# An adder convolution whose sums of maxima move from VectorE to accumulating DMAs

## The chip, the cores and the metric

The kernel runs on one core of a Trainium2 chip, as one launch. The metric is the device time of that launch in microseconds (us). The engines are named as in the profile: PE multiplies matrices, PEld loads its weights, DVE (VectorE) and ACT (ScalarE) work element by element, POOL (GpSimd) and SP issue DMAs here, and 16 DMA engines move what they issue.

## The reference

Four layers follow each other on `x` of 8 images, 64 channels, 128 x 128 pixels, each as `x = x + layer(groupnorm(x))`. The change touches the first, an adder convolution: a 3 x 3 convolution with the absolute difference in place of the product, then bias and relu.

```python
patches = conv_general_dilated_patches(x, (3, 3), (1, 1), [(1, 1), (1, 1)])
P = patches.transpose(0, 2, 3, 1).reshape(-1, C * 9)
wf = w.reshape(O, -1)
def per_out(wrow, bi):
    return relu(bi - abs(P - wrow[None, :]).sum(-1))
```

So each of 64 output channels needs, at each pixel, 9 x 64 absolute differences of the input and a weight, and their sum. The other three layers are a spline activation, a wavelet convolution and a nearest codebook vector.

## The kernel before

**Tiling.** Two images share the 128 partitions (64 channels each), which makes four pairs of images. `layer0` handles one pair: four chunks of 32 rows, padded to 34 x 130 in SBUF, and for each chunk four groups of 16 output channels. One chunk and one group are a pass; a pair has 16 passes. Within a pass each output channel `m` needs its nine taps. A tile is the term of one or more taps for one `m`: a 128 x 4096 buffer, of which PE sums the channels with 16 matmul records (line 722).

**Kinds of tile.** A string of letters gives each `m` its tiles in order. `A` is one tap's absolute difference, one ACT operation (line 653). The others use |x - w| = 2 max(x, w) - x - w, with a matmul weight of 2 (`sel2`); the linear rest is added per pass by the matmuls of `linear` (line 616). `D` is one tap's maximum, one DVE operation (line 655). `C` is the sum of two taps' maxima: the maximum of the first (655) and two fused maximum-and-add operations of half a tile each (659). `T` is the same with three taps. A fused tile saves PE a tile and costs DVE three operations instead of two. `PLANS` holds four tables of such strings; `PLANS[0]` is used in all 16 passes of the first pair and in the last two passes of each later pair, whose other passes use plans 3, 1 and 2 because layers two and three of the pair before run beside them (`layer2_beside`, `layer3_beside`).

**Order.** The order on PE, ACT and DVE is the written one (`manual_schedule`); POOL's and SP's is left to the framework's scheduler. The loop at line 703 takes two tiles a step. Before each tile's matmuls it fills every buffer in `free` with the next tiles' terms (`terms`, lines 705 to 710), so the number of buffers is the distance that DVE and ACT may run ahead of PE. After the matmuls the buffer goes back (line 723). Then come the step's chores: load of the next chunk into one of the free buffers 24 steps before it begins, its normalization 8 steps before, `relu` at the end of a pass, eight residual adds after it (line 633, DMAs from POOL that accumulate 64 KB each into `y`), and `finish` 14 steps after the end (statistics and stores). In the first pair there are seven buffers of the padded size beside `x0`, which holds the first chunk; one of the eight always holds the current chunk.

**Setup.** Before the first pair, `raw_norm` loads the first pair in eight pieces of 1 MB through three buffers, DVE takes their statistics, and then the weights of the later layers are prepared.

Of the kernel before, what the change touches and what calls it, by code (L numbers as in the profile page):

```python
# [21 lines left out]
P = 128  # L22
C = 64
# [3 lines left out]
RA = 32  # L27
# [8 lines left out]
M = 16  # L36
OG = C // M
NP = H // RA * OG
LATER = 8
BUFS_ALONE, BUFS_BESIDE = 8, 7  # L40

SPAN = {"A": 1, "D": 1, "C": 2, "T": 3}
PLANS = (
    (
        "AADDACAD",
        "DADAACAD",
        "DADACADA",  # L50
        "ADADDCAA",
        "DAACADAD",
        "DDAADCAA",
        "DADDAADC",
        "DADAADDDD",
    ),
    (
        "ACAACAA",
# [28 lines left out]
        "ACAAAT",  # L87
        "AAAACAC",
        "AAADCAC",
    ),  # L90
)
assert all(sum(SPAN[k] for k in kinds) == 9 for plan in PLANS for kinds in plan)
# [8 lines left out]
class Net:  # L101
# [21 lines left out]
    def setup(self, w0, b0, coef, sbase, ssp, bias1, dw_w, dw_b, pw_w, pw_b, cv_w, cv_b, embed):  # L123
# [54 lines left out]
        self.ones = ct([C, P], "ones")  # L178
        nc.gpsimd.memset(self.ones, 1.0)
        self.mhalf = ct([P, 1], "mhalf")  # L180
        nc.gpsimd.memset(self.mhalf, -0.5)

# [6 lines left out]
        self.b0 = ct([P, len(PLANS), OG], "b0")  # L189
        with tc.tile_pool(name="setup", bufs=1) as sp, tc.tile_pool(name="setup_ps", bufs=2, space=PSUM) as pp:  # L190
            w0o = sp.tile([P, OG, C, 9], F32, name="w0o")
            braw = sp.tile([P, OG], F32, name="braw")
            with nc.allow_non_contiguous_dma("weights, once"):
                for i in range(2):
# [167 lines left out]
            self.b2c = ct([P, 2], "b2c")  # L362
            for oab in range(2):
                bp = pp.tile([P, 1], F32, name="bp", tag="tp")
                nc.tensor.matmul(bp, self.gam[0:C, oab, :], self.ones[:, 0:1], start=True, stop=True)
# [15 lines left out]
            nc.tensor.matmul(ep, self.ones, esq, start=True, stop=True)  # L381
            self.esq_half = ct([P, NE], "esq_half")
            nc.scalar.mul(self.esq_half, ep, 0.5)

# [43 lines left out]
    def raw_norm(self, pair, mr):  # L428

        stats = self.stats_tile()  # L430
        with self.tc.tile_pool(name="raw", bufs=3) as pool:
            for j in range(NCH):
                t = pool.tile([P, R * W], F32, name="raw")
                self.nc.sync.dma_start(out=t, in_=self.x_dram[pair][:, j * R * W : (j + 1) * R * W])
                yield
                self.tile_stats(stats, 4 * j, t)
                yield
        with self.tc.tile_pool(name="raw_ps", bufs=1, space=PSUM) as pp:
            yield from self.group_norm_steps(stats, mr, pp)
# [103 lines left out]
    def layer0(self, pair, mr, stats, bufs, beside):  # L543
# [9 lines left out]
        with ExitStack() as ctx:  # L553
            bp = ctx.enter_context(tc.tile_pool(name="l0_bufs", bufs=1))
            sp = ctx.enter_context(tc.tile_pool(name="l0", bufs=1))
            pp = ctx.enter_context(tc.tile_pool(name="l0_ps", bufs=1, space=PSUM))
            ctx.enter_context(tc.manual_schedule(engines={ET.PE, ET.Activation, ET.DVE}))
            free = deque(bp.tile([P, (RA + 2) * (W + 2)], F32, name=f"buf{n}") for n in range(bufs - 1))
            held, xps, pss, sums, sxs, sts, ys, xr = {}, {}, {}, {}, {}, {}, {}, []
# [6 lines left out]
            def load(j):  # L566
                held[j] = free.popleft()
                xps[j] = self.load_chunk(pair, j, held[j])

            def pad(j):  # L570
                at = self.chunk_rows(xps[j], j)[2]
                self.normalize(at, at, mr)

            def tap(j, t, h=None):
                lo, n = (0, RA) if h is None else (h * RA // 2, RA // 2)
# [71 lines left out]
            def terms(p, m, kind, ts):  # L647
                j, o = divmod(p, OG)
                w = self.w0[:, o * M + m, :]
                buf = free.popleft()  # L650
                ab = buf[:, 0 : RA * W].rearrange("p (r w) -> p r w", w=W)
                if kind == "A":
                    nc.scalar.activation(ab, tap(j, ts[0]), AF.Abs, bias=w[:, ts[0] : ts[0] + 1], scale=-1.0)  # L653
                else:
                    nc.vector.tensor_scalar(ab, tap(j, ts[0]), w[:, ts[0] : ts[0] + 1], None, ALU.max)  # L655
                    for h in range(2):
                        at = ab[:, h * RA // 2 : (h + 1) * RA // 2, :]
                        for t in ts[1:]:
                            nc.vector.scalar_tensor_tensor(at, tap(j, t, h), w[:, t : t + 1], at, ALU.max, ALU.add)  # L659
                return buf, ab  # L660

            tiles, first = [], [0]
            for p in range(NP):
# [33 lines left out]
            held[0] = self.x0  # L697
            xps[0] = self.x0.rearrange("p (r w) -> p r w", w=W + 2)
            chores[-24].clear()
            chores[-8].clear()  # L700
            made = {}
            coming = iter(range(len(tiles)))
            for step in range(max(chores) + 1):
                for n in range(2 * step, min(2 * step + 2, len(tiles))):
                    while free:
                        k = next(coming, None)
                        if k is None:
                            break
                        p, m, kind, ts = tiles[k]
                        made[k] = terms(p, m, kind, ts)  # L710
                        if k - LATER in first[OG::OG]:
                            free.append(held.pop(p // OG - 1))
# [3 lines left out]
                    buf, ab = made.pop(n)  # L716
                    sel = self.sel if kind == "A" else self.sel2
                    for q in range(2):
                        for g in range(NG):
                            rhs = ab[:, RA // 2 * q + 4 * g : RA // 2 * q + 4 * g + 4, :]  # L720
                            at = pss[p][2 * M * g : 2 * M * (g + 1), q, :]
                            nc.tensor.matmul(at, sel[:, M - 1 - m : 3 * M - 1 - m], rhs, start=(n == first[p]), stop=(n + 1 == first[p + 1]))  # L722
                    free.append(buf)
                for f, *a in chores.pop(step, ()):
                    f(*a)

# [579 lines left out]
    def run(self):  # L1306
        tc = self.tc
        mr, later = self.mr0, None
        for pair in range(self.n_pairs):
            last = pair + 1 == self.n_pairs  # L1310
            stats, nxt = self.stats_tile(), self.mr_tile()
            raw, count = (iter(()), 2) if last else (self.raw_norm(pair + 1, nxt), 2 * NCH + 8)
            plans = [3] + [1] * 7 + [2] * 6 + [0] * 2 if later else [0] * NP
            counts = [TILES[n] // 2 if n else 0 for n in plans[:-2]] + [count // 2] * 2
            if later is None:
                self.layer0(pair, mr, stats, BUFS_ALONE, lambda p: (plans[p], raw, counts[p]))
            else:
                with tc.tile_pool(name="between", bufs=1) as bp:
                    between = bp.tile([P, NCH * 4, 6], F32, name="between")
                    steps = chain(self.layer2_beside(later, between, sum(counts[:8])), self.layer3_beside(between, pair - 1, sum(counts[8:-2])), raw)  # L1320
                    self.layer0(pair, mr, stats, BUFS_BESIDE, lambda p: (plans[p], steps, counts[p]))
            if last:
                self.first.close()
            else:
# [42 lines left out]
```

## Time and profile before

| | us |
|---|---|
| median of three runs | 19169.5 (19165.1 to 19175.5) |
| the profiled execution: span from first to last instruction | 19147.4 |
| first matmul of the first pair | 143.7 |
| relu (line 620) of its first and last pass, 15 passes apart | 378.3 and 3788.2 |
| one residual add in the first pair, issue to landing, median | 3.9 |

The span is that of one execution, and the run's time also holds what lies around it, some 22 us. In the page, busy time is the share in which an engine worked on an instruction; the records of PE overlap, so its busy share says where PE had work and not that it worked at its peak. A group's row gives busy time, the mean of one, and the idle time before it with what ended that idle time. The chain of waits is followed back from the last instruction, at each step to what released it.

### The profile page before, as it was taken

How to read it: one execution, taken by the hardware profiler on the slowest of the kernel's cores; microseconds unless marked ns; L12 is line 12 of the kernel's file. 1: busy time of each engine (PE TensorE's matmuls, PEld its weight loads, DVE VectorE, ACT ScalarE, POOL GpSimd, SP SyncE). 2: the span in 40 equal slices, each digit the busy share in tenths (PEclk: the TensorE clock that was granted, in tenths of full speed). 3: DMA queues.
4: the chain of work that ended last, by engine and by line, in shares of the span. 5: the costliest groups of instructions: out<-in, count | busy, mean ns of one | idle time of the engine just before them, and what ended most of it. 6: DMA issues, size and time to landing. Idle time of an engine off the chain costs nothing.

```text
span 19147.4 us, 330733 instructions
## 1 busy us (share of the span) xinstructions
PE 18332.0 (96%) x146698; PEld 5818.3 (30%) x146698; DVE 17951.2 (94%) x13918; ACT 17340.8 (91%) x6457; POOL 2778.2 (15%) x1663
## 2 busy tenths in 40 slices
PE   8999999999999999999999999999999999999977
PEld 2333233232233222222222322222232323222263
DVE  8999999989999999998999999999899999999867
ACT  7999999889999999988999999998899999999803
POOL 0000000000000244300000034420000003442005
PEclk9999999999999999999999999999999999999986
DMA  2000000121111001021111100002011110000231
GB/s 66 6 11 10 6 10 8 40 68 32 40 34 33 25 18 29 25 61 48 34 42 30 33 21 24 23 28 78 29 35 41 35 34 16 22 25 13 62 96 39
DMA packets 425513, 636.07 MB, mean 33 GB/s; under 512 B 65168, under 2 KB 314640, under 8 KB 399120
## 3 DMA queue, kind: packets, MB, share of 16 engines
q1 hardware_dynamic: 368272, 549.81, 9.5%
q0 software_dynamic: 55808, 65.11, 1.9%
q8 instruction: 1149, 18.83, 0.4%
q14 instruction: 284, 2.33, 0.0%
HBM read 485.16 MB, written 129.54 MB: 32 GB/s over the span
## 4 chain that ended last, share of the span: by engine, by line
PE 53%; DVE 28%; issue 10%; ACT 8%; DMA 1%; SPq 0%; POOL 0%; DVEq 0%; ACTq 0%; POOLq 0%
PE ps L722 39%; DVE buf L655 12%; DVE buf L659 9%; ACT buf L653 7%; PE cv L1139 5%; PE pa L818 2%; PE pb L818 2%; DVE dw L1116 1%; DVE nd L1264 1%; DVE ix L1266 1%; DVE dw L897 1%; PE py L1162 1%; DVE x L655 1%; ACT t L1254 1%; PE pd L1252 1%
## 5 line engine op out<-in xcount | busy, mean ns | idle before, releaser
L722 PE MATMUL ps<-buf,sel 128*32 128x512 f32 x116336 | 13030.5, 597 | 371.1 <-DVE buf L659 234.2
L653 ACT ACTIVATE buf<-buf,w 128x4096 f32<-128x4096 f32 x1980 | 7213.9, 3710 | 301.8 <-PE ps L722 295.3
L653 ACT ACTIVATE buf<-x,w 128x4096 f32<-128x4096 f32 x1938 | 7046.2, 3710 | 347.0 <-PE ps L722 288.0
L722 PEld LDWEIGHTS ps<-buf,sel 128*32 128x32 f32 x116336 | 3625.9, 110 | 9365.5 <-issue 7898.4
L655 DVE TENSOR_SCALAR buf<-buf,w 128x4096 f32<-128x4096 f32 x1795 | 4162.2, 2356 | 188.7 <-PE ps L722 187.5
L655 DVE TENSOR_SCALAR buf<-x,w 128x4096 f32<-128x4096 f32 x1558 | 3639.5, 2366 | 287.4 <-PE ps L722 271.2
L659 DVE SCALAR_TENSOR_TENSOR buf<-buf,w,buf 128x2048 f32<-128x2048 f32 x1262 | 2913.4, 2348 | 22.9
L659 DVE SCALAR_TENSOR_TENSOR buf<-x,w,buf 128x2048 f32<-128x2048 f32 x1072 | 2475.3, 2349 | 19.7
L1267 POOL DMA_INDIRECT g<-in_L_conv_embed_weight,ix x768 | 1832.8, 2386 | 2840.3 <-issue 1400.3
L633 POOL DMA_DIRECT2D y<-in_x x480 | 608.8, 2099 | 9431.2 <-ACT y L620 6457.2
L1139 PE MATMUL cv<-dw,w2s 64*128 64x512 f32 x6912 | 1654.0, 606 | 3.2 <-issue 3.2
L653 ACT ACTIVATE x<-buf,w 128x4096 f32<-128x4096 f32 x396 | 1468.9, 3709 | 59.3 <-PE ps L722 59.3
L722 PE MATMUL ps<-x,sel 128*32 128x512 f32 x10832 | 1303.0, 594 | 27.1 <-DVE x L659 18.5
L1139 PEld LDWEIGHTS cv<-dw,w2s 64*128 64x128 f32 x6912 | 627.4, 186 | 1025.4 <-issue 1011.1
L655 DVE TENSOR_SCALAR x<-buf,w 128x4096 f32<-128x4096 f32 x281 | 659.9, 2348 | 24.6 <-PE ps L722 24.4
L722 PEld LDWEIGHTS ps<-x,sel 128*32 128x32 f32 x10832 | 350.8, 110 | 851.1 <-issue 747.5
L1116 DVE SCALAR_TENSOR_TENSOR dw<-sub,dws,dw 128x512 f32<-128x512 f32 (+2 forms) x768 | 574.5, 748 | 10.6
L1264 DVE CUSTOM_DVE_ANT_0 nd<-pd,t 128x512 f32<-128x512 f32 x768 | 519.8, 677 | 31.0 <-ACT t L1254 31.0
L807 DVE TENSOR_TENSOR r<-r,r 128x1024 f32<-128x1024 f32 x384 | 454.9, 1218 | 80.2 <-ACT r L806 72.2
L1266 DVE FIND_INDEX8 ix<-best,nd 128x8 uint32<-128x512 f32 x768 | 526.1, 685 | 0.1
L1252 PE MATMUL pd<-embT,xn 64*128 64x512 f32 x1536 | 490.1, 650 | 29.1 <-DVE best L1264 28.7
L1254 ACT ACTIVATE t<-esq_half,xsq 128x512 f32<-128x512 f32 x768 | 510.8, 717 | 3.1 <-DVE best L1264 3.1
(239 smaller groups left out, 7891.7 us busy)
## 6 DMA issues: line engine op xcount, KB each, us to landing
w2s<-w_dram SPq DMA_DIRECT2D x576, 192.0 KB
xd<-x_dram SPq DMA_DIRECT2D x256, 256.0 KB
x<-x_dram SPq DMA_DIRECT2D x56, 1024.0 KB
u<-u_dram SPq DMA_DIRECT2D x64, 768.0 KB
raw<-in_x SPq DMA_DIRECT2D x32, 1024.0 KB
x_dram<-y SPq DMA_DIRECT2D x512, 64.0 KB
out<-x SPq DMA_DIRECT2D x32, 1024.0 KB
y<-in_x POOLq DMA_DIRECT2D x480, 64.0 KB, 4.2
```

The source lines that it names most:

```text
L653: nc.scalar.activation(ab, tap(j, ts[0]), AF.Abs, bias=w[:, ts[0] : ts[0] + 1], scale=-1.0)
L655: nc.vector.tensor_scalar(ab, tap(j, ts[0]), w[:, ts[0] : ts[0] + 1], None, ALU.max)
L659: nc.vector.scalar_tensor_tensor(at, tap(j, t, h), w[:, t : t + 1], at, ALU.max, ALU.add)
L722: nc.tensor.matmul(at, sel[:, M - 1 - m : 3 * M - 1 - m], rhs, start=(n == first[p]), stop=(n + 1 == first[p + 1]))
L818: nc.tensor.matmul(to[images[i], q, :], dspl[:, k, ws[i], :], cubes[i][:, cols], start=(p == 0), stop=stop)
L1116: nc.vector.scalar_tensor_tensor(out, v, wt, out, ALU.mult, ALU.add)
L1139: nc.tensor.matmul(ps[:, i], weights[r, w // 3, :], v, start=(k == 0 and n == 0), stop=(k == 3 and n == 8))
L1252: nc.tensor.matmul(ps, xns[j][at, r, :], self.embT[at, :], start=True, stop=True)
L1254: nc.scalar.activation(t, self.esq_half, AF.Identity, bias=xsqs[j][:, n : n + 1])
L1264: nc.vector.tensor_tensor_reduce(nd, ps, t, 1.0, -FAR, ALU.subtract, ALU.max, mx[:, 0:1])
L1266: nc.vector.max_index(ix, mx, nd)
L1267: nc.gpsimd.indirect_dma_start(out=g[:, img, :], out_offset=None, in_=self.embed, in_offset=bass.IndirectOffsetOnAxis(ap=ix[:, 0:1], axis=0),)
```

## The change

The first pair gets a new kind of tile, `M`, also the sum of two taps' maxima. DVE computes both maxima into two buffers, and POOL issues a DMA that adds the second buffer into the first, within SBUF. `M` tiles are issued 8 places earlier than their own, and their second buffer is given back 8 tiles after use.

```diff
-BUFS_ALONE, BUFS_BESIDE = 8, 7
+AHEAD = 8
+PADDED = (RA + 2) * (W + 2)
+TERMS_ALONE, TERMS_BESIDE = 8, 5
-SPAN = {"A": 1, "D": 1, "C": 2, "T": 3}
+SPAN = {"A": 1, "D": 1, "C": 2, "M": 2, "T": 3}
 PLANS = (
     (
-        "AADDACAD",
...
+        "DAADDAMA",
+        "DACAAMD",
...
@@ raw_norm
-        with self.tc.tile_pool(name="raw", bufs=3) as pool:
+        with self.tc.tile_pool(name="raw", bufs=2) as pool:
@@ layer0
-            ctx.enter_context(tc.manual_schedule(engines={ET.PE, ET.Activation, ET.DVE}))
-            free = deque(bp.tile([P, (RA + 2) * (W + 2)], F32, name=f"buf{n}") for n in range(bufs - 1))
+            ctx.enter_context(tc.manual_schedule(engines={ET.PE, ET.Activation, ET.DVE, ET.Pool}))
+            free = deque(bp.tile([P, PADDED], F32, name="wide") for n in range(1))
+            free.extend(bp.tile([P, RA * W], F32, name=f"buf{n}") for n in range(bufs))
...
+            def release(buf):
+                if waiting and buf.shape[1] == PADDED:
+                    j = waiting.pop()
+                    held[j] = buf
+                    xps[j] = self.load_chunk(pair, j, buf)
+                else:
+                    free.append(buf)
...
+                def maxima(t):
+                    buf = free.popleft()
+                    ab = buf[:, 0 : RA * W].rearrange("p (r w) -> p r w", w=W)
+                    nc.vector.tensor_scalar(ab, tap(j, t), w[:, t : t + 1], None, ALU.max)
+                    return buf, ab
+
+                if kind == "M":
+                    (buf, ab), (other, _) = maxima(ts[0]), maxima(ts[1])
+                    into, of = (b[:, 0 : RA * W].rearrange("p (h n) -> p h n", h=2) for b in (buf, other))
+                    nc.gpsimd.dma_start(out=into, in_=of, accum_op=ALU.add, max_dma_last_dim=8192)
+                    return buf, ab, other
...
-                        (begin - 24, load),
-                        (begin - 8, pad),
+                        (begin - 32, waiting.append),
+                        (begin - 12, pad),
...
-            coming = iter(range(len(tiles)))
+            coming = deque(sorted(range(len(tiles)), key=lambda k: k - AHEAD * (tiles[k][2] == "M")))
...
-                    while free:
-                        k = next(coming, None)
-                        if k is None:
-                            break
+                    while coming and len(free) > (tiles[coming[0]][2] == "M"):
+                        k = coming.popleft()
...
-                    free.append(buf)
+                    release(buf)
+                    spare[n + LATER] = other
+                    if spare.get(n) is not None:
+                        release(spare.pop(n))
@@ run
-            plans = [3] + [1] * 7 + [2] * 6 + [0] * 2 if later else [0] * NP
+            plans = [3] + [1] * 7 + [2] * 6 + [4] * 2 if later else [0] * NP
```

The new `PLANS[0]` has 16 strings, one for each `m`: 58 `A`, 42 `D`, 6 `C` and 16 `M` in a pass, 122 tiles. The old one has 60 `A`, 56 `D` and 14 `C`, 130 tiles; it stays as `PLANS[4]` for the last two passes of the later pairs. The term buffers lose the padding, so that nine fit (eight small ones and one of two padded buffers, of which the other holds the chunk); the next chunk is loaded into the padded buffer that comes free. POOL's order becomes the written one too. In setup, the tile `ones` moves from the constants to a pool that is closed after setup.

More of the change, by code (lines that the diff above doesn't have):

```diff
@@ L39 @@
 LATER = 8
-BUFS_ALONE, BUFS_BESIDE = 8, 7
-SPAN = {"A": 1, "D": 1, "C": 2, "T": 3}
+AHEAD = 8
+PADDED = (RA + 2) * (W + 2)
+TERMS_ALONE, TERMS_BESIDE = 8, 5
+SPAN = {"A": 1, "D": 1, "C": 2, "M": 2, "T": 3}
 PLANS = (
     (
-        "AADDACAD",
[L49 to L55, printed above, removed]
+        "DAADDAMA",
+        "DACAAMD",
+        "ADAADADM",
+        "DDAAAMAD",
+        "ACAMADD",
+        "ADADAMDA",
+        "DAADMAC",
+        "AAMDADDA",
+        "AMADDADA",
+        "ACMADAA",
+        "DADAMDAD",
+        "DDAADMAA",
+        "DADMACA",
+        "DAAMDADA",
+        "ACMDAAD",
+        "DAADDAAM",
     ),
@@ L89 @@
         "AAADCAC",
+    ),
+    (
+        "AADDACAD",
+        "DADAACAD",
+        "DADACADA",
+        "ADADDCAA",
+        "DAACADAD",
+        "DDAADCAA",
+        "DADDAADC",
+        "DADAADDDD",
     ),
@@ L177, in setup @@
         nc.vector.tensor_reduce(self.reorder[:, :, M : 2 * M], ident.rearrange("p (g i m) -> p i m g", g=NG, i=2), AX.X, ALU.add)
-        self.ones = ct([C, P], "ones")
-        nc.gpsimd.memset(self.ones, 1.0)
         self.mhalf = ct([P, 1], "mhalf")
@@ L191, in setup @@
             w0o = sp.tile([P, OG, C, 9], F32, name="w0o")
+            ones = sp.tile([C, P], F32, name="ones")
+            nc.gpsimd.memset(ones, 1.0)
             braw = sp.tile([P, OG], F32, name="braw")
@@ L364, in setup @@
                 bp = pp.tile([P, 1], F32, name="bp", tag="tp")
-                nc.tensor.matmul(bp, self.gam[0:C, oab, :], self.ones[:, 0:1], start=True, stop=True)
+                nc.tensor.matmul(bp, self.gam[0:C, oab, :], ones[:, 0:1], start=True, stop=True)
                 nc.vector.tensor_tensor(self.b2c[:, oab : oab + 1], bp, b2[:, 1, oab : oab + 1], ALU.add)
@@ L380, in setup @@
             ep = pp.tile([P, NE], F32, name="ep", tag="ep")
-            nc.tensor.matmul(ep, self.ones, esq, start=True, stop=True)
+            nc.tensor.matmul(ep, ones, esq, start=True, stop=True)
             self.esq_half = ct([P, NE], "esq_half")
@@ L556, in layer0 @@
             pp = ctx.enter_context(tc.tile_pool(name="l0_ps", bufs=1, space=PSUM))
-            ctx.enter_context(tc.manual_schedule(engines={ET.PE, ET.Activation, ET.DVE}))
-            free = deque(bp.tile([P, (RA + 2) * (W + 2)], F32, name=f"buf{n}") for n in range(bufs - 1))
-            held, xps, pss, sums, sxs, sts, ys, xr = {}, {}, {}, {}, {}, {}, {}, []
+            ctx.enter_context(tc.manual_schedule(engines={ET.PE, ET.Activation, ET.DVE, ET.Pool}))
+            free = deque(bp.tile([P, PADDED], F32, name="wide") for n in range(1))
+            free.extend(bp.tile([P, RA * W], F32, name=f"buf{n}") for n in range(bufs))
+            padded, waiting, held, xps, pss, sums, sxs, sts, ys, xr = set(), [], {}, {}, {}, {}, {}, {}, {}, []
             plan = [beside(p)[0] for p in range(NP)]
@@ L564, in banks @@
                 return pp.tile([P, 2, NE], F32, name=f"ps{p % 2}", tag=f"ps{p % 2}")
-            def load(j):
-                held[j] = free.popleft()
-                xps[j] = self.load_chunk(pair, j, held[j])
+            def release(buf):
[5 more added lines that the diff above has]
+                    free.append(buf)
             def pad(j):
@@ L572, in pad @@
                 self.normalize(at, at, mr)
+                padded.add(j)
             def tap(j, t, h=None):
@@ L649, in terms @@
                 w = self.w0[:, o * M + m, :]
+                assert j in padded
+                def maxima(t):
[8 more added lines that the diff above has]
+                    return buf, ab, other
                 buf = free.popleft()
@@ L659, in terms @@
                             nc.vector.scalar_tensor_tensor(at, tap(j, t, h), w[:, t : t + 1], at, ALU.max, ALU.add)
-                return buf, ab
+                return buf, ab, None
             tiles, first = [], [0]
@@ L698, in layer0 @@
             xps[0] = self.x0.rearrange("p (r w) -> p r w", w=W + 2)
-            chores[-24].clear()
-            chores[-8].clear()
-            made = {}
-            coming = iter(range(len(tiles)))
+            chores[-32].clear()
+            chores[-12].clear()
+            padded.add(0)
+            made, spare = {}, {}
+            coming = deque(sorted(range(len(tiles)), key=lambda k: k - AHEAD * (tiles[k][2] == "M")))
+            n_made = 0
             for step in range(max(chores) + 1):
                 for n in range(2 * step, min(2 * step + 2, len(tiles))):
-                    while free:
-                        k = next(coming, None)
-                        if k is None:
-                            break
+                    while coming and len(free) > (tiles[coming[0]][2] == "M"):
+                        k = coming.popleft()
                         p, m, kind, ts = tiles[k]
                         made[k] = terms(p, m, kind, ts)
-                        if k - LATER in first[OG::OG]:
-                            free.append(held.pop(p // OG - 1))
+                        if n_made - LATER in first[OG::OG]:
+                            release(held.pop(p // OG - 1))
+                        n_made += 1
                     p, m, kind, ts = tiles[n]
@@ L715, in layer0 @@
                         pss[p] = banks(p)
-                    buf, ab = made.pop(n)
+                    buf, ab, other = made.pop(n)
                     sel = self.sel if kind == "A" else self.sel2
@@ L1312, in run @@
             raw, count = (iter(()), 2) if last else (self.raw_norm(pair + 1, nxt), 2 * NCH + 8)
-            plans = [3] + [1] * 7 + [2] * 6 + [0] * 2 if later else [0] * NP
+            plans = [3] + [1] * 7 + [2] * 6 + [4] * 2 if later else [0] * NP
             counts = [TILES[n] // 2 if n else 0 for n in plans[:-2]] + [count // 2] * 2
             if later is None:
-                self.layer0(pair, mr, stats, BUFS_ALONE, lambda p: (plans[p], raw, counts[p]))
+                self.layer0(pair, mr, stats, TERMS_ALONE, lambda p: (plans[p], raw, counts[p]))
             else:
@@ L1320, in run @@
                     steps = chain(self.layer2_beside(later, between, sum(counts[:8])), self.layer3_beside(between, pair - 1, sum(counts[8:-2])), raw)
-                    self.layer0(pair, mr, stats, BUFS_BESIDE, lambda p: (plans[p], steps, counts[p]))
+                    self.layer0(pair, mr, stats, TERMS_BESIDE, lambda p: (plans[p], steps, counts[p]))
             if last:
```

## The prediction, made before the change was run

> **What bounds the kernel now.** The change's new plan runs only in the first pair, so after the page's first rows I read the table of windows for one undisturbed pass there (645.76 us, where the chain of waits starts a run of matmuls, to the same place one pass later), then the chain, then timelines of DVE, ACT and POOL, and the DMA view of that stage.
>
> ```profile
> PE 18332.0 (96%) x146698; PEld 5818.3 (30%) x146698; DVE 17951.2 (94%) x13918; ACT 17340.8 (91%) x6457; POOL 2778.2 (15%) x1663
> ...
> core 0: us, PE busy (x) PEld busy (x) DVE busy (x) ACT busy (x) POOL busy (x), PEclk, DMA share, GB/s
> 645.76:870.98 225.22, 225.22 (x2089) 68.17 (x2092) 224.29 (x101) 218.19 (x62) 12.63 (x8) 1.00 0.03 6
> ```
>
> A pass takes 225.2 us. PE is busy in all of it, DVE in all but 0.9, ACT in all but 7; the clock is 1.00 and the DMA engines are nearly idle (0.03). The chain agrees:
>
> ```profile
> 645.76 223.30 PE ps L722 x2080
> 869.07 1.91 PE ps L616 x4
> ```
>
> 2080 matmul records are one pass of 130 tiles: 223.30/130 = 1.718 us a tile, then 1.91 for the linear part, and nothing else. PE sets the pass; DVE and ACT follow so closely that taking tiles from PE alone would gain 1 us.
>
> **The passes' sums.** Old plan per pass: 60 A, 56 D, 14 C = 130 tiles. New: 58 A, 42 D, 6 C, 16 M = 122 tiles.
>
> ```profile
> 604.97 9.13 DVE L655 TENSOR_SCALAR buf<-x,w 128x4096 f32<-128x4096 f32 x4
> 614.14 4.61 DVE L659 SCALAR_TENSOR_TENSOR buf<-x,w,buf 128x2048 f32<-128x2048 f32 x2
> ...
> 829.65 21.77 ACT L653 ACTIVATE buf<-x,w 128x4096 f32<-128x4096 f32 x6
> ```
>
> Operations overlap at their ends, so I take the step, not the mean: (9.13 - 2.35)/3 = 2.26 us for a maximum and as much for a fused half; (21.77 - 3.71)/5 = 3.61 for an absolute value.
> - PE: 8 tiles fewer, 225.2 - 8 x 1.718 = **211.5**.
> - DVE: D 1, C 3, M 2 operations: 98 become 42 + 18 + 32 = 92; 224.3 - 6 x 2.26 = **210.7**.
> - ACT: 218.2 - 2 x 3.61 = **211.0**.
>
> The three end within 0.8 us. If nothing else changed a pass would gain 13.7 us.
>
> **What an M costs.** Its sum is no longer made on DVE: POOL issues a DMA that adds one 2 MB buffer into another. No such DMA is in the trace; the nearest row is the residual add of line 633 (64 KB, accumulating).
>
> *Generation on POOL.*
>
> ```profile
> 604.83 4.84 POOL L633 DMA_DIRECT2D y<-in_x  x2 [212.98 <-ACT y L620]
> ...
> 614.19 1.63 POOL L633 DMA_DIRECT2D y<-in_x  x2
> ```
>
> The first two lie beside the four maxima: 4.84 us, ending just after each maximum's end. The last two lie beside fused halves: 1.63 us, started 0.51 apart. So POOL cannot write its descriptors while a maximum (line 655) runs. The Trainium skill, "SBUF — State Buffer", section "Who interferes with whom", says the same of DVE's two-port modes (whoever comes first holds the shared pair for the whole instruction) and advises against hiding such DMAs under DVE. This rule speaks against the change: of the new 92 operations 80 are maxima. Read as starvation, an M would wait out a row of four maxima, 9 us; by the row it waits for the end of one: 2.3 + 0.1 = 2.4 us. An M has 256 rows of 8 KB against 32; gathers of 128 rows (line 1267) take 0.94 us at least, so (0.94 - 0.51)/96 = 4.5 ns a row, 1.5 us for 256, which fits under that one maximum. I take **2.4**; ends 1.5 and 4.7 (two maxima). In return POOL can hold DVE up: beside gathers a maximum takes 2.51 instead of 2.35 us (at 6796.2), 0.16 each. 16 x 0.16 = 2.6 brings DVE to **213.3**, which then is the floor of a pass; ends 0 and 16 x 1.5 = 24.
>
> *Transfer.*
>
> ```profile
> q1 hardware_dynamic: 11696, 18.86, 2.4%
> q0 software_dynamic: 4608, 6.30, 1.5%
> ```
>
> q0 in this stage is the residual adds alone. Of its 4608 packets 3072 carry 2 KB: 1.5% of 16 engines x 2912 us is 699 us, 0.227 each, first packets of short bursts included; their median in the packet records is 0.176, where plain 2 KB packets (q1) have 0.098 and plain 8 KB packets 0.313. So an accumulating packet costs about two plain ones, and an 8 KB one 0.63. An M has 256, 16 on each engine: 10.0, with a slow first packet **10.3 us**. Ends: 5.0 (plain), 14.5 (64 times 0.227). The skill would have it otherwise: "DMA: Bandwidth & Descriptors", section "Anatomy of one DMA — SWDGE (gpsimd) path", gives 2.0 us + bytes/436 GB/s, 6.8 for 2 MB; an M would then never be late. That fit is for copies; the row with the add in it decides. The engines are busy 16 x 10.3 = 165 of some 220 us, so the queue itself does not bound.
>
> *Lateness.* From the second maximum: 2.4 generation, 0.7 to the first packet (POOL done 607.4, first packets 608.1), 10.3, 0.3 to land = 13.7. With its two maxima (4.5) an M needs **18.2 us** from the time its buffers come free. What it has: I walked the loop's free list tile by tile. Seven term buffers let ordinary tiles be written 6 tiles ahead; now nine do, but each M holds two, and its second for 8 tiles longer: ordinary tiles fall to 4 ahead, and an M, queued 8 places early, comes out 11.3 ahead (10 to 12). 11.3 x 1.72 = 19.4 us. The cover is 1.2 us, and it is used up by whatever comes first: a C before it on DVE (6.8 us), the residual adds (8 x 2 packets in the same queue), the chunk load. PE waits in order, and with 4 tiles of lead beside three engines at 211 a lost us is not regained. I take half of the 16 as late by 0.9: 7.2 us. **A pass: 213.3 + 7.2 = 220.5, gain 4.7; 16 passes: -75.**
>
> **The other edits.**
> - Raw buffers 3 to 2, setup: eight 1 MB loads, each then read by four statistics (18.31 us for 30, so 2.4 a chunk). With two buffers a load is issued only after the statistics two chunks before, and needs 2.6 us on the engines plus about 2 to land: some 3.5 us a chunk instead of 2.4 for the last six. The queue's later weight loads stand behind them. **+6**; ends 0, +9. In the passes the raw loads are 17 us apart and hidden.
> - Fifth plan in setup: 16 small POOL copies of 0.14 us and some ten small DVE operations, before POOL's idle 35 us: 0.
> - Loads of a chunk wait for the one free wide buffer, asked for 32 steps ahead, not 24; normalization at 12, not 8. In pairs two to four there are six term buffers as before, but one is lent out for 16 steps (32 tiles) longer at nine chunk ends: **+5**; ends 0, +15.
> - POOL in written order: the residual adds go out one a step, the last 5 steps before the statistics that read them (10 tiles, 17 us), against 2 + 3.7 us to land, or 14 behind an M. Hidden; without that cover DVE stands at line 643 once a pass. Pairs two to four keep their plans: 0.
>
> Sum: -75 + 6 + 5 = -64 against this execution (span 19147.4; the runs' median 19169.5 lies 22 us above, launch and end outside the span). Forecast **19105**.
>
> **Rivals.**
> - *Always in time*: 10 us or less per transfer and an even order. Pass 213.3: -190 + 11, **18990**. For it: each sum above is near its low end. Against it: a cover of 1.2 us.
> - *Gain eaten*: packets of 2 KB at 0.176, 64 per engine: 11.3 us, need 19.2, cover 0.2; all 16 late by 0.6: pass 222.9, -37 + 11, **19144**, no difference.
> - *The lead is too short* (slower): once every M is late, its place in the order, tied to PE, sets the pace: 11.3 tiles take as long as an M needs, so a pass takes 122/11.3 = 10.8 times that. It beats 225.2 from 20.9 us on, that is a transfer of 13 us or a second maximum in the generation's way. With 11.3 and 4.7: 21.5 us, pass 232, +112 + 11: **19290**; with 14.5 and 2.4: 22.4, pass 242, 19450. For it: all of POOL's unknowns lengthen; against: the packet records.
>
> **How the numbers follow.** Forecast 0.34, always in time 0.12, gain eaten 0.19, too short 0.35. A measurement of this kernel can tell about 0.2% (38 us) from no change: faster 0.46, same 0.19, slower 0.35. The likeliest case's own range is 18990 to 19130. The whole range goes from 18980 to 19400: it leaves out the upper end of the last rival and little below.
>
> **What would show it.** Right: passes of 219 to 222 us between line 620's activations; line 722 waiting in part for a DMA `buf<-buf`; about 2.4 us of POOL and 13 to 14 us to landing per M; q0 at 70 to 80% in the first pair; first matmul some 6 us later; the pairs after it within 15 us. Wrong: landing above 16 us, maxima longer than 2.6 us, or passes at 213.

## The result, and the profile after

| | before | after |
|---|---|---|
| median of four runs | 19172.3 us | 19465.7 us |
| ratio, 95% interval | | 1.0158 [1.0144, 1.0173] |
| first matmul of the first pair | 143.7 | 149.9 |
| from there to the 16th relu (the first pair) | 3644.5 | 3919.2 |
| from there to the 64th relu (pairs two to four) | 14119.2 | 14143.7 |
| from there to the end of the span | 1240.1 | 1251.7 |

The changed kernel is slower by 293 us, and above the upper end of the forecast range. The last four rows are read from the two traces: +6 us ahead of the first pair, +275 in it, +25 in the pairs after it, +12 at the end. They add up to 317 and not to 293, because the old trace is of a faster execution than the four that were timed: in every run that lists both, the time lies under 2 us above the span, so the 22 us between the old kernel's span and its median are no launch time. The end belongs to the chip and not to the change: in the runs below it takes 1258 to 1262 us where the old kernel takes 19177 or 19179, and 1240 to 1242 where that takes 19154 or 19155. So the first pair holds the answer.

The old kernel's page, its slices of PE and of the DMA engines:

```profile
PE   8999999999999999999999999999999999999977
...
DMA  2000000121111001021111100002011110000231
```

The page of the changed kernel, its rows of engines, of slices and of queues:

```profile
PE 18248.3 (94%) x144652; PEld 5740.2 (29%) x144652; DVE 17760.2 (91%) x13828; ACT 17240.3 (89%) x6425; POOL 3565.8 (18%) x1935
...
PE   7989888899999999999999999999999999999977
...
DMA  7878877851111100002111100102111110000221
...
q0 software_dynamic: 125440, 602.00, 17.2%
```

The work that was to go is gone: 2046 matmul records fewer in the page, close to 16 passes x 8 tiles x 16 records. But PE, which had all nines in the first pair, now has sevens and eights there, and the DMA engines stand at seven and eight tenths where they had been almost idle. The table of windows for one of the better passes (233.4 us from relu to relu):

```profile
core 0: us, PE busy (x) PEld busy (x) DVE busy (x) ACT busy (x) POOL busy (x), PEclk, DMA share, GB/s
649.30:882.70 233.40, 219.09 (x1992) 63.39 (x1984) 216.13 (x96) 211.58 (x60) 50.64 (x24) 0.99 0.83 150
```

All three engines now wait, PE for 14 us. Whom PE waited for, from 400 to 3700 us (waits of the matmuls and of their weight loads, total us, times, longest):

```profile
PEld ps L762 <- DMA buf<-buf: 339.1, 140, 17.5
PE ps L762 <- DMA buf<-buf: 218.0, 115, 16.6
PEld ps L762 <- DVE buf L694: 74.1, 109, 2.5
PEld ps L762 <- ACT buf L692: 69.9, 97, 9.0
```

The two rows of a matmul overlap and are not to be added; either way the wait of the first pair is one for the accumulating DMA, and its longest is 17 us. Where a 17 us wait comes from is in the timelines around 611 us, first DVE, then POOL (start, duration):

```profile
606.26 4.61 DVE L681 TENSOR_SCALAR buf<-x,w 128x4096 f32<-128x4096 f32 x2
610.79 4.61 DVE L694 TENSOR_SCALAR buf<-x,w 128x4096 f32<-128x4096 f32 x2
615.32 2.35 DVE L694 TENSOR_SCALAR wide<-x,w 128x4096 f32<-128x4096 f32 x1
617.58 4.61 DVE L681 TENSOR_SCALAR buf<-x,w 128x4096 f32<-128x4096 f32 x2
622.10 6.87 DVE L694 TENSOR_SCALAR buf<-x,w 128x4096 f32<-128x4096 f32 x3
```

```profile
611.18 19.34 POOL L687 DMA_DIRECT2D buf<-buf  x2 [19.33 <-DVE buf L681]
```

The maxima of an M end at 610.87 and POOL begins to generate its DMA at 611.18. DVE goes on with eight more maxima, each starting as the last one ends, and POOL's first generation lasts until 629.29, just after the last of them: 18.11 us. DVE stops only because it has no buffer left, for PE stands still waiting for this very DMA. The usual case, 115 us later, again DVE and POOL:

```profile
726.35 2.34 DVE L694 TENSOR_SCALAR buf<-x,w 128x4096 f32<-128x4096 f32 x1
728.61 2.51 DVE L694 TENSOR_SCALAR wide<-x,w 128x4096 f32<-128x4096 f32 x1
```

```profile
726.73 2.27 POOL L687 DMA_DIRECT2D buf<-buf  x1 [11.47 <-DVE buf L681]
```

POOL waits for the end of one maximum and writes while the next, 2.51 instead of 2.35 us long, waits for it. By the records, 11 of the 256 generations last longer than 5 us (nine of them 13.6 or 18.1), and all 11 belong to the last M of a pass. The rest has a median of 2.27. From the end of a generation an M takes 13.3 us to land (median; 12.4 to 24.1, the long ones behind another M in the queue).

PE starts four matmul records every 0.43 us. What the steps from 250 us to the end of the pair have over that sums to 508 us of pauses, 33 before: 160 in 11 pauses over 8 us, 66 in 16 of 3 to 8, and 281 in short ones. The 475 us more, less the 220 us of matmuls that went, are most of the 275.

### The profile page after: what moved, and what is told of

Same layout as the page of the kernel before. It is cut to its first block, busy times and chain, and to the rows that moved or that the text cites. A ratio compares the mean times of both kernels' runs of the same rounds, so it can differ in the third digit from the quotient of the medians.

```text
span 19464.5 us, 327057 instructions
## 1 busy us (share of the span) xinstructions
PE 18248.3 (94%) x144652; PEld 5740.2 (29%) x144652; DVE 17760.2 (91%) x13828; ACT 17240.3 (89%) x6425; POOL 3565.8 (18%) x1935
## 3 DMA queue, kind: packets, MB, share of 16 engines
q14 instruction: 287, 2.35, 0.0%
## 4 chain that ended last, share of the span: by engine, by line
PE 39%; DVE 28%; issue 14%; ACT 10%; DMA 7%; POOL 1%; SPq 0%; DVEq 0%; ACTq 0%; POOLq 0%; another core or an unknown queue 0%
PE ps L762 26%; DVE buf L694 11%; DVE buf L698 8%; ACT buf L692 7%; PE cv L1182 5%; DMA buf<-buf 5%; PE pa L861 2%; PE pb L861 2%; ACT wide L692 1%; DVE buf L681 1%; DVE dw L1159 1%; DVE ix L1309 1%; DVE nd L1307 1%; ACT t L1297 1%; DVE dw L940 1%
## 5 line engine op out<-in xcount | busy, mean ns | idle before, releaser
L762 PE MATMUL ps<-buf,sel 128*32 128x512 f32 x107776 | 12231.0, 600 | 668.2 <-DMA buf<-buf 259.0
L692 ACT ACTIVATE buf<-x,w 128x4096 f32<-128x4096 f32 x1829 | 6673.2, 3710 | 459.3 <-PE ps L762 449.0
L692 ACT ACTIVATE buf<-wide,w 128x4096 f32<-128x4096 f32 x1784 | 6500.9, 3708 | 448.7 <-PE ps L762 433.5
L694 DVE TENSOR_SCALAR buf<-x,w 128x4096 f32<-128x4096 f32 x1474 | 3462.7, 2372 | 334.9 <-PE ps L762 319.4
L694 DVE TENSOR_SCALAR buf<-wide,w 128x4096 f32<-128x4096 f32 x1420 | 3318.7, 2366 | 302.3 <-PE ps L762 301.8
L698 DVE SCALAR_TENSOR_TENSOR buf<-wide,w,buf 128x2048 f32<-128x2048 f32 x1064 | 2456.5, 2348 | 19.5
L692 ACT ACTIVATE wide<-x,w 128x4096 f32<-128x4096 f32 x333 | 1235.2, 3709 | 128.0 <-PE ps L762 71.2
L692 ACT ACTIVATE x<-wide,w 128x4096 f32<-128x4096 f32 x336 | 1245.7, 3707 | 64.7 <-PE ps L762 64.7
L762 PE MATMUL ps<-wide,sel 128*32 128x512 f32 x8544 | 1036.8, 600 | 102.3 <-ACT wide L692 46.8
L687 POOL DMA_DIRECT2D buf<-buf x202 | 523.7, 2594 | 2445.8 <-DVE buf L681 2117.4
L681 DVE TENSOR_SCALAR buf<-x,w 128x4096 f32<-128x4096 f32 x229 | 528.8, 2345 | 141.7 <-PE ps L762 141.3
L681 DVE TENSOR_SCALAR buf<-wide,w 128x4096 f32<-128x4096 f32 x229 | 528.8, 2346 | 133.0 <-PE ps L762 131.9
```

The lines of the kernel that those rows point to most:

```text
L681: nc.vector.tensor_scalar(ab, tap(j, t), w[:, t : t + 1], None, ALU.max)
L687: nc.gpsimd.dma_start(out=into, in_=of, accum_op=ALU.add, max_dma_last_dim=8192)
```

## The experiments

Theory A: the M tiles' sums come late, by their transfer and by the generations that POOL cannot get done. Theory B: what surrounds them costs the time, that is the four tiles of lead, maxima in pairs, the buffers, POOL's written order. Twelve kernels were run, each against the changed one unless said otherwise, each once (e10_best six times). In the table, "first pair" is from the first matmul to the 16th relu, "pairs 2 to 4" from there to the 64th, "end" what follows, and "old" the old kernel's time on the same chip in the same round. As the chips differ by some 20 us at the end, the first pair's column compares the kernels better than the whole time.

| run | time, us | old | first matmul | first pair | pairs 2 to 4 | end |
|---|---|---|---|---|---|---|
| before | 19172 | | 143.7 | 3645 | 14119 | 1240 |
| after | 19466 | 19172 | 149.9 | 3919 | 14144 | 1252 |
| e1_old_plan | 19193 | 19179 | 146.0 | 3637 | 14147 | 1262 |
| e2_no_add | 19111 | 19179 | 150.8 | 3549 | 14150 | 1260 |
| e3_gap | 19310 | 19179 | 150.3 | 3745 | 14155 | 1258 |
| e5_back | 19312 | 19179 | 150.8 | 3751 | 14149 | 1259 |
| e4_half | 19094 | 19154 | 151.3 | 3549 | 14149 | 1242 |
| e6_gap_back | 19149 | 19154 | 150.2 | 3609 | 14148 | 1241 |
| e7_gap_back_ahead | 19114 | 19154 | 150.0 | 3566 | 14155 | 1240 |
| e8_eight | 19285 | 19154 | 147.2 | 3745 | 14151 | 1240 |
| e10_best | 19095 | 19155 | 149.6 | 3567 | 14136 | 1240 |
| e11_gap_before | 19304 | 19155 | 151.1 | 3762 | 14148 | 1241 |
| e9_ahead12 | 19257 | 19155 | 151.7 | 3718 | 14146 | 1241 |
| e12_one_gap | 19553 | 19177 | 151.1 | 3990 | 14152 | 1258 |

**The old table in the new kernel.**

```diff
-            plans = [3] + [1] * 7 + [2] * 6 + [4] * 2 if later else [0] * NP
-            counts = [TILES[n] // 2 if n else 0 for n in plans[:-2]] + [count // 2] * 2
+            plans = [3] + [1] * 7 + [2] * 6 + [4] * 2 if later else [4] * NP
+            counts = [TILES[n] // 2 if n and later else 0 for n in plans[:-2]] + [count // 2] * 2
```

> The changed kernel with the old table in the first pair's passes (no M tile); buffers, written POOL order, two raw buffers and load times stay as changed. If the loss is the M tiles' own (their sums come late): passes near 225 us again, the whole at 19180 to 19215 us, above the old kernel by the 6 us of setup and up to 35 us that the trace shows after the first pair. If the loss lies in what surrounds them (term buffers without padding, the one wide buffer, POOL's order): passes above 232 us and 19300 us or more.

19193: the first pair takes 3637 us, 7 less than in the old kernel. The loss is the M tiles' own, as A had it; pairs two to four lose their 27 us without any M tile too.

**Without the sums.**

```diff
-                    nc.gpsimd.dma_start(out=into, in_=of, accum_op=ALU.add, max_dma_last_dim=8192)
```

The second maximum of each M is left out of the sum.

> The changed kernel without the accumulating DMA of the M tiles: the second maximum of each pair is computed and left out of the sum; order and buffers stay. If late sums are the cause: passes of 216 to 219 us (three engines at 211 us of work, four tiles of lead), 15.5 passes of 244.6 shorter by 26 to 28 us, the whole near 19050 us. If the short lead of ordinary tiles or the pairs of maxima cost the time: passes stay above 230 us, 19250 us or more.

The first pair is 370 us shorter: so much did the DMAs cost. But six of the 15 passes from relu to relu take 219.4 us and the others 218 to 227, so A's size was off by 60 us (19050 was written): a pass takes some 8 us more than the 211 of the engines' work. For whom PE waits now, from 400 to 3700 us:

```profile
PEld ps L761 <- DVE buf L693: 191.0, 209, 3.2
PEld ps L761 <- ACT buf L691: 101.8, 162, 2.1
```

These are ordinary tiles, written four tiles ahead instead of six. This is the share of B, and 95 us in the first pair is the most that the add, were it free, could bring with these buffers and this order. Whether the lead or the order of the letters makes PE wait was not tried apart.

**A small operation behind the tile that follows an M.**

```diff
+            after_m, gap = [], sp.tile([P, 1], F32, name="gap")
...
                 if kind == "M":
...
+                    after_m.append(1)
...
+                if kind != "A" and after_m:
+                    after_m.pop()
+                    nc.vector.memset(gap, 0.0)
                 return buf, ab, None
```

> The changed kernel with one small DVE operation (a memset of one column, some 0.1 us) behind the first DVE tile that follows each M. If POOL's descriptor writing loses the SBUF port at every boundary between two maxima that follow each other without a gap, the small operation lets it in: generations of 13 to 18 us (9 of 256 in the changed kernel) vanish, and of the 160 us of PE waits over 8 us some 140 go: 19310 to 19340 us. If they have another cause (instruction fetch, a full ring): they stay, and the time rises by 16 x 0.1 x 16 = 26 us to 19490.

156 us less than the changed kernel, as written, and 174 in the first pair. The view of the DMA's line, with the shortest, median and longest of its instructions in ns, in e3_gap:

```profile
L688 POOL DMA_DIRECT2D buf<-buf x202: 1194/2271/4330, 159.5 to 3874.8; - x101
```

and in the changed kernel:

```profile
L687 POOL DMA_DIRECT2D buf<-buf x202: 1194/2271/18113, 159.1 to 4048.1; - x101
```

The median is the same, the long ones are gone. So the starved generations cost 174 of the 370 us. Why it helps is another matter: the memset takes 59 ns, and the maxima keep their step of 2.26 us around it.

**The second buffer back at once.**

```diff
+BACK = 0
...
-                    spare[n + LATER] = other
+                    spare[n + BACK] = other
```

> The changed kernel with an M's second buffer given back with the first instead of 8 tiles later. Counted through the free list, ordinary tiles are then written 5.3 tiles ahead instead of 4.3 and M tiles 12.3 instead of 11.3, 1.8 us more cover for each M. If the lead is too short: 50 to 120 us less, 19350 to 19415 us. If the DMA engines' rate or the starved generations set the pace: within 20 us of 19466.

154 us less (168 in the first pair), more than expected, though 11 long generations stay (13.6 us now). So the buffers' lead was too short beside the long generations as well. The edit gives the ordinary tiles one more tile of lead too, and PE's waits for DVE and ACT fell with those for the DMA; the two shares were not tried apart.

**Half the transfer.**

```diff
-                    nc.gpsimd.dma_start(out=into, in_=of, accum_op=ALU.add, max_dma_last_dim=8192)
+                    nc.gpsimd.dma_start(out=into[:, 0:1], in_=of[:, 0:1], accum_op=ALU.add, max_dma_last_dim=8192)
```

The edit stands on top of that of e3_gap; half of each M's second maximum is left out of the sum.

> e3_gap with an M's DMA cut to the first half of each partition's row (128 rows of 8 KB instead of 256; the other half of the second maximum is left out of the sum). If the 11.6 us of transfer are what makes sums late: half of it leaves 5 us of cover, PE's waits for the DMA vanish, the first pair comes to 3550 to 3590 us (e3_gap 3745, without the add 3549), the whole to 19120 to 19160. If what counts is the DMA's start (POOL's wait for the port, DVE held up by it), which stays: above 19250.

The first pair takes 3549.4 us, within a microsecond of the time without the add, though every M still generates and issues a DMA; it lands 6.4 us after generation instead of 13.3. From issue to landing (with the whole transfer, in e11_gap_before, the median is 15.7):

```profile
DMA to landing us min/median/max: 7.0/8.5/13.0
```

What remained after e3_gap, 196 us, went with half of the transfer, so it was the transfer's length against the cover. (Generation has half the rows too, but is only 0.2 us shorter.) With the 174 us of the long generations this makes up the 370.

**The cures together, and one more.**

The edits of e3_gap and of e5_back in one kernel:

> e3_gap and e5_back together. If the starved generations and the short cover are two separate causes, most of both gains adds up: 156 + 154 less what both cured (the 11 long waits of e5_back were shorter by 35 us), so 19160 to 19210 us. If both work on the same waits: no better than 19290.

And on top of both:

```diff
-AHEAD = 8
+AHEAD = 10
```

> e6_gap_back with M tiles 10 places early instead of 8. More cover for the sums (some 3.4 us), but each M holds its two buffers two tiles longer, so ordinary tiles are written 4.8 instead of 5.3 ahead. If the sums' lateness is still most of what is lost: 30 to 80 us below e6_gap_back. If the ordinary tiles' lead binds by now: the same or up to 40 us above it.

19149, then 19114 with `AHEAD = 10`. In the first pair the two cures together take 310 us off, 174 + 168 less 32, about the overlap that was written: they are two causes. Two places more are worth another 42 us there. Whom PE waited for in e7_gap_back_ahead, 400 to 3700 us:

```profile
PEld ps L768 <- ACT buf L695: 225.3, 252, 2.6
PEld ps L768 <- DMA buf<-buf: 76.4, 67, 3.7
PEld ps L768 <- DVE gap L704: 56.4, 39, 3.7
```

The DMA is no longer the first of the list, and no wait for it is longer than 3.7 us. ACT, with its ordinary tiles, now is.

The same with 12:

```diff
-AHEAD = 8
+AHEAD = 12
```

> e7_gap_back_ahead with M tiles 12 places early instead of 10. In e7 PE's waits over 3 us are down to 4 in the first pair (26 us), about what is there without the add; so there is little lateness left to cure, and the buffers held longer shorten the ordinary tiles' lead: 20 to 100 us above e7 (19114). If sums were still late: below it.

With 12 places the time rises by 144 us, more than the 100 written. PE's longest wait is for ACT (7.1 us), and the greatest sums are those for DVE's and ACT's ordinary tiles (206 and 199 us). That an M holds its two buffers for longer fits this, but the number of tiles of lead alone does not explain it: counted through the free list it is 4.3, as in e2_no_add, whose first pair takes 169 us less. The cause was not tried apart. Of 8, 10 and 12 places, 10 is the best.

**Half the M tiles.** On top of e6_gap_back, eight of the 16 strings of the first pair's table lose their M, and POOL's order stays written only where the first pair runs alone:

```diff
-        "DAADDAMA",
+        "AADDACAD",
         "DACAAMD",
-        "ADAADADM",
+        "DADACADA",
         "DDAAAMAD",
-        "ACAMADD",
+        "DAACADAD",
         "ADADAMDA",
-        "DAADMAC",
+        "DADDAADC",
         "AAMDADDA",
-        "AMADDADA",
+        "AADDACAD",
         "ACMADAA",
         "DADAMDAD",
-        "DDAADMAA",
-        "DADMACA",
+        "ADADDCAA",
+        "DAACADAD",
         "DAAMDADA",
-        "ACMDAAD",
+        "DADDAADC",
         "DAADDAAM",
...
-            ctx.enter_context(tc.manual_schedule(engines={ET.PE, ET.Activation, ET.DVE, ET.Pool}))
+            ctx.enter_context(tc.manual_schedule(engines={ET.PE, ET.Activation, ET.DVE} | ({ET.Pool} if bufs == TERMS_ALONE else set())))
```

> e6_gap_back with 8 M in a pass instead of 16 (60 A, 48 D, 10 C, 8 M, 126 tiles: PE 218.4, ACT 218.2, DVE 216.5 us a pass), and POOL's order left to the scheduler in pairs two to four as in the old kernel. If DMA time and buffers held by M tiles are what is lost: passes near 220 us, first pair 3540 to 3580. If any M costs as much as it saves: 3640 or more. After the first pair: if POOL's written order costs the 36 to 50 us that all changed kernels show there, they go (15359 us from its last relu to the end, as before); if the wide buffer or the two raw buffers do, they stay (15395 to 15410).

A miss. With half the M tiles the first pair takes 3745 us, 136 more than e6_gap_back with all of them. Of these, 110 are the four tiles a pass that PE has back (4 x 1.718 x 16). The rest is that its pauses did not shrink: 229 us (13 in four over 3 us, 216 in short ones) against 206, for DVE and ACT as well as for the DMA. The strings had been put together from the two tables with an eye to sums alone; whether the order of the letters makes the short waits was not tried. How many M tiles are best was not settled by it. In the same run POOL's order was left to the scheduler in the later pairs: 14151 us for them against 14148 in e6_gap_back, so the written order is not what costs the time there.

**Two controls on the memset.**

In front of an M's two maxima:

```diff
+            gap = sp.tile([P, 1], F32, name="gap")
...
                 if kind == "M":
+                    nc.vector.memset(gap, 0.0)
```

> Control for e3_gap: the changed kernel with the same 16 small DVE operations a pass, each in front of an M's two maxima instead of behind the tile that follows them. If the small operation helps because it breaks the row of maxima while POOL waits, this one does nothing for POOL: generations over 5 us stay (8 or more), 19460 to 19500 us. If it helps by shifting the phase of DVE against POOL, whatever its place: the long generations vanish here too, near 19310.

Once, where the pair begins:

```diff
             plan = [beside(p)[0] for p in range(NP)]
+            gap = sp.tile([P, 1], F32, name="gap")
+            nc.vector.memset(gap, 0.0)
```

> The changed kernel with a single small DVE memset in each pair, ahead of all tiles, instead of 16 a pass. e3_gap and e11_gap_before cured the long generations from two places, and their row of maxima kept its step of 2.26 us, so a broken row is not what did it. If the small operations must stand near each M (they change what the sequencers do around it), the long generations stay: 8 or more over 5 us, 19460 to 19500. If any shift of DVE's instruction stream is enough: they vanish, near 19305.

The DMA's line in e11_gap_before, then in e12_one_gap:

```profile
L689 POOL DMA_DIRECT2D buf<-buf x202: 1194/2271/4325, 160.4 to 3892.4; - x101
L689 POOL DMA_DIRECT2D buf<-buf x202: 1194/2271/20096, 160.3 to 4120.5; - x101
```

In front of the two maxima it works as well as behind the next tile. This rules out that it opens a gap for POOL: 239 of the 256 generations end with the first maximum behind the M, as the usual ones do in the changed kernel, and no memset starts while any of them runs. One memset a pair does not work: 16 generations over 5 us, and 71 us more in the first pair than in the changed kernel, some 14 for each further one (the changed kernel's own four runs spread over 44 us, so part of this may be chance). So 16 a pass, near the M tiles, help and one a pair does not; whether their place or their number counts was not tried. What they change in the contest for POOL's turn stays open.

**A version that beats both.**

The edits of e7_gap_back_ahead, and with them the wide buffer asked for and padded in the first pair as in the changed kernel and in the later pairs as late as before, and three raw buffers for the statistics:

```diff
-            for _ in self.raw_norm(0, self.mr0):
+            for _ in self.raw_norm(0, self.mr0, 3):
...
+            lend, early = (32, 12) if bufs == TERMS_ALONE else (24, 8)
...
-                        (begin - 32, waiting.append),
-                        (begin - 12, pad),
+                        (begin - lend, waiting.append),
+                        (begin - early, pad),
```

> e7_gap_back_ahead with two small edits whose effects fall in different stages: three raw buffers again in setup alone, and in pairs two to four the next chunk's buffer asked for 24 steps ahead and normalized 8 ahead, as in the old kernel. First matmul at 144 us instead of 150. If the longer lending of the one wide buffer costs the 30 us after the first pair, that stage falls to 15360 to 15370 us and the whole to about 19080; if not, it stays at 15390 and the whole is near 19108. Either way 0.2 to 0.5% below the old kernel.

19094.6 us (six runs) against 19155.3 (ten runs of the old kernel): 0.9967 [0.9955, 0.9979], a small gain but clear of noise. Pairs two to four take 14136 us, 8 to 19 less than in the other changed kernels, so the earlier loads are part of what those pairs lost. The first matmul did not move.

## Why the prediction was wrong

The forecast had the first pair shorter by 75 us, and it is longer by 275. Of these 350 us, 124 were lost before an M cost anything, and 226 in what the M tiles cost.

**The engines' sums** held as sums: 220 us of matmuls went from the first pair. That a pass would follow them did not. "If nothing else changed" it was to gain 13.7 us, 219 in 16 passes; without the add it gained 95 in all (e2_no_add). The prediction saw the ordinary tiles fall from 6 to 4 ahead, but let this count only where an M is late, and put nothing for the ordinary tiles themselves. They cost some 8 us a pass: e2_no_add, with no M to wait for, takes about the 220.5 us a pass that were forecast with the late M tiles in them.

**What an M costs** was put at 9 us a pass (211.5 to 220.5), 144 in the pair. It was 370, 174 by generation and 196 by the transfer.

**Generation, 2.4 us.** As a median it was right (2.27, and 0.16 of delay for the next maximum, as read from the old trace). What failed is the step from that row to all 256 generations, with two maxima as its upper end: 11 lasted 3 to 8 maxima. The old trace could not tell this. Its row of residual adds from 600 to 3700 us looks as if it could:

```profile
L633 POOL DMA_DIRECT2D y<-in_x x112: 782/1968/9382, 604.8 to 3562.4; - x112
```

But the 9.38 us are a queue. Four maxima begin at 3562.59; at 3565.1, 3567.4 and 3569.6 us, each just after one of them, three, two and one of the adds are left:

```profile
3562.59 9.12 DVE L655 TENSOR_SCALAR buf<-buf,w 128x4096 f32<-128x4096 f32 x4
3561.40 10.39 POOL L633 DMA_DIRECT2D y<-in_x  x3
3561.91 9.89 POOL L633 DMA_DIRECT2D y<-in_x  x2
3562.41 9.38 POOL L633 DMA_DIRECT2D y<-in_x  x1
```

POOL got one in at each end. Counted from the end of the one ahead of it, none of the old kernel's 480 residual adds took over 3.0 us; the M of 18.11 us had none ahead. The Trainium skill, "SBUF — State Buffer", section "Who interferes with whom", has the shared pair held for a whole instruction and the other side blocked for as long. The median agrees with this, one maximum's end; a turn lost at eight ends in a row goes beyond it. Eleven of 256 were enough, since PE takes its tiles in order.

**Transfer, 10.3 us** was mis-sized. The smallest 8 KB packet took 0.627 us, exactly the two plain packets of the estimate, but the mean was 0.726: 11.6 us of every engine per M and 12.2 from first to last packet. With it an M needs 4.5 + 0.3 + 2.3 + 13.3 = 20.4 us, not 18.2, against the 19.4 that the walk through the free list gave. The 196 us are this: e4_half takes the excess away and the lateness with it.

**Lateness, half of the M tiles by 0.9 us.** The cover of 1.2 us was rightly called thin and then given a mild price. By the packet records no M of the changed kernel landed less than 19.7 us after its first maximum began, so all were over the 19.4 that they have on average, and the mean is some 22 us with the long generations in it. Once the need exceeds the cover each late M moves all that follows. The rival "the lead is too short" had that mechanism: put 22 us into its 10.8 times and a pass takes 238 us, where 244.6 was the mean measured. Its dearest case, 19450, was left outside the range.

**Setup, +6**: right in size (6.2), wrong in cause. With two raw buffers the statistics end 10 us later (the last statistic starts at 54.1 us instead of 44.1), but DVE's first maximum waits for a weight DMA that ends later still. e10_best has three again and starts at 149.6. DVE begins 2.8 us later than in the old kernel, and with three buffers still 2.4. Its first instructions show 4.5 us more:

```profile
142.73 2.35 DVE L681 TENSOR_SCALAR wide<-x,w 128x4096 f32<-128x4096 f32 x1 [5.88 <-DMA u_dram<-u]
145.00 2.35 DVE L681 TENSOR_SCALAR buf<-x,w 128x4096 f32<-128x4096 f32 x1
147.26 7.03 DVE L694 TENSOR_SCALAR buf<-x,w 128x4096 f32<-128x4096 f32 x3
```

Issued 8 places early, the first M's maxima (681) stand ahead of the first tile that PE needs (694). That this tile is now a maximum and no longer an absolute value gives 1.3 us back.

**Later pairs, +5**: 25 to 36 us against the old trace. Asking for the wide buffer as late as before gave part of it back (17 are left in e10_best); POOL's order gave none (e8_eight). The remainder was not found.

## What to carry to other kernels

When a result that PE takes in order is handed to a DMA, compare its whole latency, measured to landing, with the lead that the buffers allow, tile by tile; a mean rate below the engines' capacity says nothing (78% of it here was slow, 85% in e10_best fast). Ask what the added buffers and places cost the ordinary tiles before the new work costs anything: a kernel that leaves the new work out shows it. When records of a queue overlap, count each from the end of the one ahead of it; a long record may be a queue and no lost turn. And give a buffer back as soon as its last reader is done: eight tiles of caution cost 154 us here.

## What the runs showed of the hardware

- An accumulating DMA within SBUF moved 8 KB packets in 0.63 us at best and 0.73 on average; 2 MB on 16 engines took 11.6 us of each. With half as much per DMA (e4_half) the mean packet took 0.65; why was not tried.
- Descriptor writing for 256 rows took 1.19 us at best, 2.27 behind one maximum, and could lose its turn at up to eight maxima in a row, whose ends looked no different in the records from those at which it won. In the old kernel, with 32 rows each, it never took over 3.0 us. Sixteen memsets of 59 ns a pass, near the M tiles, ended the long ones without a change in DVE's step; the mechanism is open.
